# Cross attention's last statistics and projections, and integer attention's third output buffer

## The chip, the cores and the metric

The kernel runs on one core of one Trainium2 chip. The metric is device time in microseconds of one launch, the median of several runs. One run is taken with the hardware profiler; the profile and the trace are of that execution. Engines are named as in the profile: PE is TensorE (PEld its weight loads), DVE is VectorE, ACT is ScalarE, POOL is GpSimd, SP issues the DMAs.

## The reference

A decoder of two levels on x of shape (8, 512, 256), all in float32. Each step adds to x what a block computes of the layer-normalised x:

```python
x = x + L0_attn(layernorm(x))          # self attention, softmax over the queries
x = x + L0_xattn(layernorm(x), ctx)    # 16 heads, scores + adj, integer mask
x = x + L0_ffn(layernorm(x))           # two layers of local attention and gated ffn
x = x + L1_attn(layernorm(x))          # integer attention, values rounded to 8 bits
x = x + L1_xattn(layernorm(x), ctx)    # media attention, 8 heads, masked keys
x = x + L1_ffn(layernorm(x))           # mixture of 8 experts, one per row
```

The change lies in the second and the fourth step. The second, for each batch:

```python
scores  = Q K^T / sqrt(16) + adj
scores  = where(mask == 0, -inf, scores)
out     = softmax(scores) V            # 16 heads of 16
x       = x + out Wo^T + bo
```

The fourth quantises inputs, scores, probabilities and outputs to integers with global scales. Its last product is `attn_int @ wo_int.T + bias_int`, multiplied by a scale for each output column, and added to x.

## The kernel before

x stays in SBUF as 32 tiles of 128 rows by 256, four to a batch. The program is written by hand as stages; a scheduler orders each engine's queue at compile time, by the order in the program, its own model of durations, the tiles' buffers and the dependences. `tc.issue_after(ins)` makes what is written inside it stand behind `ins` on its engine; `high_priority` brings it forward. At run time each engine goes through its queue in order.

**Self attention** (`stage_self_attention`) goes over 8 batches: scores, exponentials, then `weigh`, which for each of four row tiles takes a reciprocal (L1412), a scale (L1413) and a product (L1415) on VectorE and adds the tile to x on GpSimd (L1417). `means(b)` (L1419) computes mean and inverse deviation of the batch's new x for cross attention: for each of four tiles `bn_stats` and `bn_aggr` (L143, L144), then a chain of small instructions on 128x4 elements (L148, L149, L1477 to L1481, L1424), copied into `self.x_ln`. It runs a batch late; the last batch's stands behind the loop (L1445). The bounds check `sa_ok` (L1447 to L1451) ends the stage.

**Cross attention** (`stage_cross_attention`) prepares batch 0 during self attention; its main loop then has 128 steps and two more, 16 steps to a batch. Step i issues, for four heads and one tile of 128 keys: `scores(i)` (four matmuls in two PSUM tiles, L1724), `soften(i)` (two exponentials on ScalarE, L1735, and two multiplications by the mask's share on VectorE, L1736), and `weigh(i - 2)` (four matmuls, L1752). Between them comes side work: the next batch's `prepare` (keys, values, queries, normalised rows: one group a step), and `later`, a list of jobs with due steps: reciprocals of the softmax sums, which go through DRAM (`inverted`, L3330), the multiplication on GpSimd (L1769), the output projection `project_out` (L1785 and L1790) and the statistics of its result. `paced` puts a job behind the VectorE instruction `marks[-2]`, that is, behind the multiplications of the step before. PSUM has six banks for scores, one for `po`, and one, `pj`, that all side work shares. `project_out` multiplies into `pj` and VectorE adds the bank to x:

```python
x = self.x[:, b * NST + i, :]
nc.vector.tensor_tensor(x, x, ps[:, :C], ALU.add)
```

`padded(j, pool)` allocates and clears one of two value buffers, padded to 32 columns a head (GpSimd memset, L1558); odd batches use the second. Toward the end (from step n - 13) the first local attention's preparation (`turn`, `project`, `rotate`, L1881 to L1953) runs between the steps.

**Integer attention** (`stage_quantized_attention`) ends with pool `qa5`: eight activations (L2744) round the attention output, transposes follow (L2748), and after the second of four pairs `bias_parts` splits the bias into three bfloat16 rows on VectorE (L2415 to L2424) and `orow`, the column scales, is written. `bias_parts` allocates its two working rows in a pool of its own. Then for each of 8 batches: 12 matmuls into one of two PSUM tiles (L2764, L2767), `project`, which does a piece of the media attention's keys and values (L2799, stored by a DMA from `kv_o`), a product by `orow` on VectorE into `qa_o` (L2772) and the addition to x (L2773), on GpSimd for batches 2, 4, 6 and on VectorE for the rest. `qa_o` has two buffers of the pool. Batch 0's statistics for the next stage come in between (`twice_normal`), and the others' products stand behind them. The media attention (L2933, L2943, L2963) is the next stage. Its weights are loaded by `load_media_attention` long before.

Of the kernel before, what the change touches and what calls it, by code (L numbers as in the profile page):

```python
# [27 lines left out]
F32 = mybir.dt.float32  # L28
# [1249 lines left out]
class FastDecoder(Decoder):  # L1278
# [31 lines left out]
    def stage_self_attention(self, w, ahead):  # L1310
# [7 lines left out]
        with self.tc.tile_pool(reuse_waits="tile", name="sa", bufs=2) as pool, self.tc.tile_pool(  # L1318
# [97 lines left out]
                    x = self.x[:, at, :]  # L1416
                    nc.gpsimd.tensor_tensor(x, x, o, ALU.add)  # L1417

            def means(b):  # L1419

                x = self.x[:, b * NST : (b + 1) * NST, :]
                at = slice(b * NST, (b + 1) * NST)
                for kept, new in zip(self.x_ln, self.ln_stats(pool, lambda i: [x[:, i, :]], NST, "x_ln")):
                    nc.vector.tensor_copy(kept[:, at], new)  # L1424
# [8 lines left out]
            for b in range(B):  # L1433
# [8 lines left out]
                if b > 0:  # L1442
                    means(b - 1)
                    ahead.step(3)
            means(B - 1)  # L1445
            ok = self.alloc(pool, [P, NT], F32, "sa_ok", bufs=1)
            nc.vector.tensor_scalar(ok, inv, 1.0 / self.SHIFTED_MAX, 1.0 / self.SHIFTED_MIN, ALU.max, ALU.min)  # L1447
            nc.vector.tensor_tensor(ok, ok, inv, ALU.is_equal)  # L1448
# [79 lines left out]
    def stage_cross_attention(self, ahead):  # L1528
# [27 lines left out]
        def padded(j, pool):  # L1556
            v = self.alloc(pool, [P, NST, 16, 32], F32, f"x_v{j}", bufs=1)
            nc.gpsimd.memset(v, 0.0)  # L1558
            nc.gpsimd.memset(v[:, :, :, 0:1], 1.0)
            return v  # L1560
# [30 lines left out]

        def prepare(b):

            d = held[b] = {"v": v_pad[b % 2]}
            own = (first, second)[b % 2]

            def load():
                d["ctxT"] = self.alloc(first, [P, 2, S], F32, "x_ctxT")
                nc.sync.dma_start(
                    d["ctxT"], t["ctxT"].rearrange("(k p) n -> p k n", p=P)[:, :, b * S : (b + 1) * S]  # L1600
                )
                d["mask"] = self.alloc(first, [P, NST, S], I32, "x_mask", bufs=1)
                nc.sync.dma_start(d["mask"], t["x_maskT"][b].rearrange("(k p) q -> p k q", p=P))
                nc.sync.dma_start(
                    self.slots[b * CAP : (b + 1) * CAP, :].rearrange("(p r) c -> p r c", p=P),
                    empty.unsqueeze(1).broadcast_to([P, CAP // P, self.WIDE]),
                )

            def share(k):
                if k == 0:  # L1610
                    d["share"] = self.alloc(own, [P, NST, S], F32, f"x_share{b % 2}", bufs=1)
                nc.vector.scalar_tensor_tensor(
                    d["share"][:, k, :], d["mask"][:, k, :], 0.0, adj[:, k, :], ALU.not_equal, ALU.mult
                )

            x = self.x[:, b * NST : (b + 1) * NST, :]
            normals = [
                lambda i=i: self.normalize(d["xn"][:, i, :], x[:, i, :], self.x_ln, b * NST + i)
                for i in range(NST)
            ]  # L1620

            def behind():
                nc.gpsimd.tensor_tensor(x, x, bias.unsqueeze(1).broadcast_to([P, NST, C]), ALU.add)

            def rows():
                d["xn"] = self.alloc(first, [P, NST, C], F32, "x_xn", bufs=1)
                d["xnT"] = self.alloc(first, [P, 2, S], F32, "x_xnT", bufs=1)
                d["q"] = self.alloc(own, [P, 2, 2, S], F32, f"x_q{b % 2}", bufs=1)
                d["k"] = self.alloc(own, [P, 2, S], F32, f"x_k{b % 2}", bufs=1)

            def turn(c):
                ps = self.pj()
                for i in range(NST):
                    nc.tensor.transpose(
                        ps[:, i * P : (i + 1) * P], d["xn"][:, i, c * P : (c + 1) * P], self.ident
                    )
                nc.scalar.copy(d["xnT"][:, c, :], ps)

            def project(wt, src, g):
                ps = self.pj()  # L1640
                for k in range(2):
                    nc.tensor.matmul(
                        ps, wt[:, k, g * P : (g + 1) * P], src[:, k, :], start=(k == 0), stop=(k == 1)
                    )
                return ps

            def queries(g):
                ps = project(wq, d["xnT"], g)
                for e in range(2):
                    nc.scalar.activation(  # L1650
                        d["q"][:, e, g, :], ps, AF.Identity,
                        bias=qb[:, 2 * e + g : 2 * e + g + 1], scale=qsc[:, e : e + 1],
                    )

            def keys(g):
                ps = project(wk, d["ctxT"], g)
                nc.scalar.activation(d["k"][:, g, :], ps, AF.Identity, bias=bk[:, g : g + 1])

            def values(i):
                ps = self.pj()  # L1660
                for k in range(2):
                    nc.tensor.matmul(
                        ps[:, :C], d["ctxT"][:, k, i * P : (i + 1) * P], wv[:, k, :],
                        start=(k == 0), stop=(k == 1),
                    )
                nc.scalar.copy(
                    d["v"][:, i, :, 1:17], ps[:, :C].rearrange("p (h d) -> p h d", d=16)
                )

            K = [lambda g=g: keys(g) for g in range(2)]  # L1670
            V = [lambda i=i: values(i) for i in range(NST)]
            M = [lambda i=i: share(i) for i in range(NST)]
            T = [lambda c=c: turn(c) for c in range(2)]
            Q = [lambda g=g: queries(g) for g in range(2)]
            yield [load, rows]
            yield []
            yield [K[0]]
            yield []
            yield [K[1]]
            yield [normals[0], normals[1], V[0]]  # L1680
            yield [normals[2], normals[3], V[1]]
            yield [behind, T[0], M[0]]
            yield [T[1], V[2]]
            yield [Q[0], M[1]]
            yield [Q[1]]
            yield [V[3], M[2]]
            yield []
            yield [M[3]]
# [8 lines left out]
        with self.tc.tile_pool(reuse_waits="tile", name="xa", bufs=2) as pool, self.tc.tile_pool(  # L1697
# [2 lines left out]
            second = pool  # L1700
            self.pj = lambda: self.alloc(psum, [P, 512], F32, "pj")
            self.reserve(psum, ("pj", [P, 512], 1), ("po", [P, 512], 1), ("sc", [P, 2, 512], 3))
            v_pad.append(padded(1, pool))

            marks = []

            def paced(thunk):
# [74 lines left out]
            def project_out(b, i):  # L1782
                ps = self.pj()
                for g in range(2):
                    nc.tensor.matmul(  # L1785
                        ps[:, :C], held[b]["oT", g][:, i * P : (i + 1) * P], wo[:, g, :],
                        start=(g == 0), stop=(g == 1),
                    )
                x = self.x[:, b * NST + i, :]
                nc.vector.tensor_tensor(x, x, ps[:, :C], ALU.add)  # L1790
                if i == 0:
                    rows = self.x[:, b * NST : (b + 1) * NST, :]
                    held[b]["norm"] = self.ln_pieces(pool, rows, lambda i: rows[:, i, :], "lt_ln")
                means, roots, normals = held[b]["norm"]
                means[i]()
                if i == NST - 1:
                    nc.sync.dma_start(self.away[b], self.x[:, b * NST : (b + 1) * NST, :])
                    for k, root in enumerate(roots):
                        later.add(1 + k, lambda root=root: paced(root))
                    for k, normal in enumerate(normals):  # L1800
                        later.add(5 + k // 2, lambda normal=normal: paced(normal))
# [11 lines left out]
            for i in range(n + 2):  # L1813
# [13 lines left out]
                later.tick(2)  # L1827
                if i == 1:
                    ahead.step()
                if i == n - 14:  # L1830
                    early.close()
                if i >= n - 13:
# [571 lines left out]
        nc.vector.tensor_tensor(hi, hi, lo, ALU.max)  # L2404
        nc.vector.tensor_tensor(q["xtop"][:, b * NST : (b + 1) * NST], hi, rstd, ALU.mult)

    def bias_parts(self, out, rb, inv, tag):

        nc, part = self.nc, self.ident[:, :3]
        n = rb.shape[1]  # L2410
        with self.tc.tile_pool(reuse_waits="tile", name=tag, bufs=1) as tmp:
            v = self.alloc(tmp, [P, n], F32, tag + "_v")
            acc = self.alloc(tmp, [P, n], F32, tag + "_a")
            piece = self.alloc(tmp, [P, n], BF16, tag + "_p")
            nc.vector.tensor_scalar(v, rb, inv, MAGIC, ALU.mult, ALU.add)  # L2415
            nc.vector.tensor_scalar(v, v, -MAGIC, None, ALU.add)
# [11 lines left out]
    def stage_quantized_attention(self, w):  # L2428
# [3 lines left out]
        with tc.tile_pool(reuse_waits="tile", name="qa", bufs=1) as pool:  # L2432
# [302 lines left out]
            with tc.tile_pool(reuse_waits="tile", name="qa5", bufs=2) as tmp, tc.tile_pool(  # L2735
                reuse_waits="tile", name="qp5", bufs=1, space=PSUM
            ) as psum:
                orow = self.alloc(tmp, [P, C], F32, "qa_orow_s", bufs=1)
                for n in range(0, 8, 2):
                    ps = [self.alloc(psum, [P, 8, P], BF16, "tr", bufs=4) for c in range(2)]  # L2740
                    for h in range(2):
# [13 lines left out]
                                ps[c][:, :, 32 * st : 32 * st + 32].rearrange("p m (k t) -> p t m k", t=B),  # L2755
                            )
                    if n == 2:
                        self.bias_parts(brow, q["rb"][:, 3 * C :], osc_inv, "qa_b")
                        nc.vector.tensor_scalar(orow, q["wsc"][:, C:], osc, None, ALU.mult)
                for b in range(B):  # L2760
                    ps = self.alloc(psum, [P, NST, C], F32, "pj", bufs=2)
# [4 lines left out]
                            )  # L2766
                        nc.tensor.matmul(ps[:, st], ones[:, :P], brow, start=False, stop=True)  # L2767
                    project(tmp, psum, "tr")
                    o = self.alloc(tmp, [P, NST, C], F32, "qa_o")
                    x = self.x[:, b * NST : (b + 1) * NST, :]  # L2770
                    with self.tc.issue_after(ahead) if b else nullcontext():
                        nc.vector.tensor_tensor(o, ps, orow.unsqueeze(1).broadcast_to([P, NST, C]), ALU.mult)  # L2772
# [6 lines left out]
        self.integers.close()  # L2779

    def load_media_attention(self):
        self.w_media = super().load_media_attention()
        return self.w_media

    def context(self, out, b):
# [815 lines left out]
```

## Time and profile before

| what | value |
|---|---|
| time, median of 3 runs | 3000.25 us |
| lowest, highest | 2999.61, 3006.4 us |
| the profiled execution's own time | 2998.56 us |
| its span in the profile | 2996.8 us |
| its mean granted TensorE clock | 0.976 |
| TensorE busy | 2811.1 us (94%) |
| VectorE busy | 2030.6 us (68%) |
| ScalarE busy | 1207.0 us (40%) |
| GpSimd busy | 377.2 us (13%) |

The span runs from the first to the last instruction of the program that was profiled; the own time of the execution is 1.76 us longer. A row of a timeline gives the start (us from the span's start), the length, the engine, the source line, the operation, what it writes and reads, and in brackets the engine's idle time before it and what ended that. Lengths of rows that are merged (x2, x6) hold all of them; on VectorE a row's length reaches a little into the next one, so that costs in a queue are taken from start to start. In stretches: self attention to 205 us, cross attention to about 690, the local transformer's two layers to 2012, integer attention to 2308, media attention to 2760, the experts to the end.

### The profile page before, as it was taken

How to read it: one execution, taken by the hardware profiler on the slowest of the kernel's cores; microseconds unless marked ns; L12 is line 12 of the kernel's file. 1: busy time of each engine (PE TensorE's matmuls, PEld its weight loads, DVE VectorE, ACT ScalarE, POOL GpSimd, SP SyncE). 2: the span in 40 equal slices, each digit the busy share in tenths (PEclk: the TensorE clock that was granted, in tenths of full speed). 3: DMA queues.
4: the chain of work that ended last, by engine and by line, in shares of the span. 5: the costliest groups of instructions: out<-in, count | busy, mean ns of one | idle time of the engine just before them, and what ended most of it. 6: DMA issues, size and time to landing. Idle time of an engine off the chain costs nothing. (4 is left out here: it accounts for less than half of the span.)

```text
span 2996.8 us, 39867 instructions
## 1 busy us (share of the span) xinstructions
PE 2811.1 (94%) x14929; PEld 1509.5 (50%) x14944; DVE 2030.6 (68%) x4514; ACT 1207.0 (40%) x1719; POOL 377.2 (13%) x357
## 2 busy tenths in 40 slices
PE   8999999988999999999999999999796999997998
PEld 5653333324555565655555565555343344444665
DVE  7458999996777883356777888549787766664110
ACT  2227777754545521135445521115263444441111
POOL 1111111100011110000011111112111012121111
PEclk9999999999999999999999999999898999998999
DMA  8011211101000010001000021010332132313331
GB/s 250 1 36 43 78 50 50 58 24 52 16 23 23 23 53 9 1 1 44 16 23 23 23 60 50 15 43 29 121 124 89 48 102 86 107 58 98 112 134 61
DMA packets 130695, 168.74 MB, mean 56 GB/s; under 512 B 51760, under 2 KB 79665, under 8 KB 128442
## 3 DMA queue, kind: packets, MB, share of 16 engines
q1 hardware_dynamic: 126394, 154.48, 16.5%
q0 software_dynamic: 4096, 11.59, 1.0%
q8 instruction: 120, 1.97, 0.3%
q14 instruction: 85, 0.70, 0.1%
HBM read 113.12 MB, written 47.50 MB: 54 GB/s over the span
## 5 line engine op out<-in xcount | busy, mean ns | idle before, releaser
L1897 PE MATMUL pj<-w,la_hT 128*128 128x512 f32 x712 | 333.1, 605 | 8.2 <-DVE x L1790 7.9
L1736 DVE TENSOR_TENSOR x_e<-x_e,x_share 128x1024 f32<-128x1024 f32 x256 | 316.8, 1280 | 14.8 <-ACT x_e L1735 14.7
L1735 ACT ACTIVATE x_e<-sc 128x1024 f32<-128x1024 f32 x256 | 249.2, 1023 | 79.1 <-PE sc L1724 79.1
L2036 DVE TENSOR_TENSOR la_e<-la_e,la_mask 128x1024 f32<-128x1024 f32 (+1 forms) x128 | 137.0, 1084 | 102.9 <-ACT la_e L2035 102.9
L1897 PEld LDWEIGHTS pj<-w,la_hT 128*128 128x128 f32 x712 | 130.3, 191 | 141.1 <-issue 117.1
L2969 ACT ACTIVATE ma_e<-sc,ma_bias 128x1024 f32<-128x1024 f32 x128 | 135.7, 1111 | 143.5 <-PE sc L2963 138.3
L2257 ACT ACTIVATE lf_gate<-pj,lf_b 128x512 f32<-128x512 f32 (+1 forms) x82 | 56.3, 687 | 320.5 <-PE pj L2236 320.5
L3344 POOL TENSOR_TENSOR la_oT<-la_o,x_wide 128x512 f32<-128x512 f32 x64 | 90.4, 1425 | 730.3 <-DMA x_wide<-invs 655.4
L2236 PE MATMUL pj<-lf_hnT,w 128*128 128x512 f32 (+1 forms) x368 | 171.9, 594 | 2.3 <-ACT lf_gate L2257 1.1
L1752 PE MATMUL po<-x_e,x_v 128*32 128x512 f32 x1024 | 138.7, 614 | 22.0 <-DVE x_e L1736 18.1
L2236 PE MATMUL sc<-lf_hnT,w 128*128 128x512 f32 x336 | 157.7, 592 | 0.0
L1724 PE MATMUL sc<-x_q,x_k 32*128 32x512 f32 x1024 | 151.8, 642 | 1.7 <-DVE sa_ok L1448 1.4
L2308 PE MATMUL po<-w,lf_hid 128*128 128x256 f32 x640 | 149.0, 379 | 0.0
L2262 DVE SCALAR_TENSOR_TENSOR lf_hid<-sc,lf_b,lf_gate 128x512 f32<-128x512 f32 x70 | 52.4, 748 | 135.9 <-PE sc L2236 134.7
L2035 ACT ACTIVATE la_e<-sc 128x1024 f32<-128x1024 f32 (+1 forms) x128 | 112.1, 918 | 45.2 <-PE sc L2027 45.2
L2027 PE MATMUL sc<-la_qkT 64*128 64x256 f32 (+1 forms) x1024 | 128.2, 378 | 0.5
L2308 PEld LDWEIGHTS po<-w,lf_hid 128*128 128x128 f32 x640 | 117.8, 190 | 21.2 <-issue 7.4
L2046 PE MATMUL po<-la_e,la_v 128*64 128x256 f32 (+1 forms) x1024 | 121.3, 363 | 7.4 <-ACT la_o L2063 6.5
L2963 PE MATMUL sc<-ma_qT,ma_kT 64*128 64x512 f32 x512 | 127.3, 615 | 0.4 <-ACT ma_e L2969 0.4
L1904 ACT ACTIVATE la_sq<-pj 128x512 f32<-128x512 f32 x120 | 71.8, 598 | 131.2 <-PE pj L1897 129.9
L2986 PE MATMUL po<-ma_e,ma_v 128*64 128x512 f32 x512 | 124.0, 605 | 0.0
L1913 DVE TENSOR_REDUCE la_ss<-la_sq 128x16 f32<-128x1024 f32 x64 | 77.6, 1213 | 66.2 <-ACT la_sq L1904 66.2
(512 smaller groups left out, 5222.7 us busy)
## 6 DMA issues: line engine op xcount, KB each, us to landing
x_wide<-invs SPq DMA_DIRECT2D x184, 128.0 KB
w<-in_f_w_dram SPq DMA_DIRECT2D x16, 1024.0 KB
kv<-kv_o SPq DMA_DIRECT2D x56, 256.0 KB
slots<-x_empty SPq DMA_DIRECT2D x8, 1028.0 KB
x_mask<-in_x_maskT_dram SPq DMA_DIRECT2D x8, 1024.0 KB
ma_kT<-kv SPq DMA_DIRECT2D x8, 1024.0 KB
ma_v<-kv SPq DMA_DIRECT2D x8, 1024.0 KB
ex_rows<-slots SPq DMA_DIRECT2D x7, 1028.0 KB
```

The lines of the kernel that those rows point to most:

```text
L1724: nc.tensor.matmul(pair[r // 2][:, r % 2, :], d["k"][rows, g, kt * P : (kt + 1) * P], d["q"][rows, e, g, :], start=True, stop=True,)
L1735: nc.scalar.activation(ex, d["e"][rest][p], AF.Exp)
L1736: nc.vector.tensor_tensor(ex, ex, d["share"][:, kt, :].unsqueeze(1).broadcast_to([P, 2, 512]), ALU.mult)
L1752: nc.tensor.matmul(d["po"][32 * r : 32 * r + 32, :], d["v"][:, kt, 8 * g + 2 * r + e, :], ex[r // 2][:, r % 2, :], start=(kt == 0), stop=( ...
L1897: nc.tensor.matmul(ps, d["hT"][:, k, i * P : (i + 1) * P], wqkv[:, k, j * S : (j + 1) * S], start=(k == 0), stop=(k == 1),)
L2027: nc.tensor.matmul(both[half][:, r, jj * 256 : jj * 256 + to - j * P], d["qkT"][rows, 4 + c, j * P : (j + 1) * P], d["qkT"][rows, c, j * P ...
L2036: nc.vector.tensor_tensor(ex[:, :, :n_cols], ex[:, :, :n_cols], mask[:, :n_cols].unsqueeze(1).broadcast_to([P, 2, n_cols]), ALU.mult,)
L2236: nc.tensor.matmul(ps[:m, :], w1[:, k, at : at + m], held[b]["hnT"][:, k, :], start=(k == 0), stop=(k == 1))
L2308: nc.tensor.matmul(ps[:, :C], held[b]["hid"][:, f, i * P : (i + 1) * P], w2[:, f, :], start=(f == 0), stop=False,)
L2963: nc.tensor.matmul(both[m // 2][:, r, :], d["k"][rows, c, kt * P : (kt + 1) * P], d["q"][rows, c, :], start=True, stop=True,)
L2969: nc.scalar.activation(ex, ps, AF.Exp, bias=bias[:, b * NST + kt : b * NST + kt + 1], scale=0.125)
L2986: nc.tensor.matmul(d["po"][64 * r : 64 * r + 64, :], d["v"][:, kt, 128 * c + 64 * r : 128 * c + 64 * r + 64], exs[m // 2][:, r, :], start= ...
```

## The change

Cross attention: the statistics of the last batch leave the end of self attention and are issued in step 2 of cross attention's loop, paced, with their small tiles in cross attention's first pool. The second padded buffer is allocated and cleared in the same step, no longer ahead of the loop. `project_out` copies its bank to SBUF on ScalarE, and VectorE adds the copy to x.

Integer attention: `qa_o` has three buffers. For the room, `orow` and the two working rows of the last `bias_parts` take the place of bias rows in `rb` that are no longer needed. The media attention's weights are loaded with the key and value weights ahead of the query weights.

```diff
-            def means(b):
+            def means(b, pool=pool):
...
-            means(B - 1)
+            self.last_means = lambda pool: means(B - 1, pool)
...
         def prepare(b):
-            d = held[b] = {"v": v_pad[b % 2]}
+            d = held[b] = {}
...
             def values(i):
+                d["v"] = v_pad[b % 2]
...
             self.reserve(psum, ("pj", [P, 512], 1), ("po", [P, 512], 1), ("sc", [P, 2, 512], 3))
-            v_pad.append(padded(1, pool))
...
                 x = self.x[:, b * NST + i, :]
-                nc.vector.tensor_tensor(x, x, ps[:, :C], ALU.add)
+                o = self.alloc(pool, [P, C], F32, "x_out")
+                nc.scalar.copy(o, ps[:, :C])
+                nc.vector.tensor_tensor(x, x, o, ALU.add)
...
                 if i == 1:
                     ahead.step()
+                if i == 2:
+                    v_pad.append(padded(1, pool))
+                    paced(lambda: self.last_means(first))
...
-    def bias_parts(self, out, rb, inv, tag):
+    def bias_parts(self, out, rb, inv, tag, room=None):
...
-            v = self.alloc(tmp, [P, n], F32, tag + "_v")
-            acc = self.alloc(tmp, [P, n], F32, tag + "_a")
+            v = room[0] if room else self.alloc(tmp, [P, n], F32, tag + "_v")
+            acc = room[1] if room else self.alloc(tmp, [P, n], F32, tag + "_a")
...
-                orow = self.alloc(tmp, [P, C], F32, "qa_orow_s", bufs=1)
+                orow = q["rb"][:, :C]
...
-                        self.bias_parts(brow, q["rb"][:, 3 * C :], osc_inv, "qa_b")
+                        self.bias_parts(brow, q["rb"][:, 3 * C :], osc_inv, "qa_b", [q["rb"][:, k * C : (k + 1) * C] for k in (1, 2)])
...
-                    o = self.alloc(tmp, [P, NST, C], F32, "qa_o")
+                    o = self.alloc(tmp, [P, NST, C], F32, "qa_o", bufs=3)
...
     def load_media_attention(self):
-        self.w_media = super().load_media_attention()
+        w, t = self.weights(), self.t
+        wkv = self.load_w(w, 1024, t["e_wkv"])
+        self.w_media = self.load_w(w, 0, t["e_wq"]), wkv, self.load_w(w, 3072, t["e_wout"])
         return self.w_media
```

## The prediction

> **What bounds the kernel now.** I read the page, then TensorE's own waits, the windows with the granted clock, and the timelines around the three places that the diff touches. TensorE is busy 94% of the span, so time is won where it waits, and lost where a wait is added.
>
> The page's first lines, then the longest waits of TensorE on the changed lines (total us, times, longest):
>
> ```profile
> span 2996.8 us, 39867 instructions
> PE 2811.1 (94%) x14929; PEld 1509.5 (50%) x14944; DVE 2030.6 (68%) x4514; ACT 1207.0 (40%) x1719; POOL 377.2 (13%) x357
> ...
> PE po L1752 <- DVE x_e L1736: 18.1, 16, 3.7
> PE pj L1897 <- DVE x L1790: 7.9, 2, 4.0
> PE pj L2764 <- DVE qa_o L2772: 6.2, 3, 2.9
> PE pj L2933 <- DVE ma_xn L157: 5.9, 1, 5.9
> PE pj L1785 <- DVE x L1790: 3.8, 7, 0.7
> ```
>
> All these together are 42 us, 1.4% of the span: the change can move no more than a few tenths of a per cent.
>
> The start of cross attention, timeline of VectorE and TensorE (start, length), then windows (PE, PEld, DVE, ACT, POOL busy, granted clock, DMA):
>
> ```profile
> 207.35 0.43 DVE L143 BATCH_NORM_STATS2 x_ln_bn<-x 128x6 f32<-128x256 f32 x1
> ...
> 211.24 6.89 DVE L1736 TENSOR_TENSOR x_e<-x_e,x_share 128x1024 f32<-128x1024 f32 x6
> 213.74 1.93 PE L1752 MATMUL po<-x_e,x_v 128*32 128x512 f32 x8 [3.69 <-DVE x_e L1736]
> 215.60 3.78 PE L1642 MATMUL pj<-x_ctxT,w 128*128 128x512 f32 x4
> ...
> 216.00:218.00 2.00, 2.00 (x3) 0.78 (x3) 2.00 (x2) 0.00 (x0) 0.00 (x0) 0.50 0.00 0
> ```
>
> The exponentials of step 0 are ready at 206.3, but VectorE is at the last statistics until 211.24; TensorE idles 3.69, and the clock is at 0.50 afterwards: the four key matmuls take 3.78 where the same ones take 1.98 at 223.69.
>
> The end of cross attention and the end of integer attention:
>
> ```profile
> 644.66 0.42 DVE L1790 TENSOR_TENSOR x<-x,pj 128x256 f32<-128x256 f32 x1 [1.40 <-PE pj L1785]
> 661.62 0.42 DVE L1790 TENSOR_TENSOR x<-x,pj 128x256 f32<-128x256 f32 x1 [0.61 <-PE pj L1785]
> 655.90 3.40 PE L1897 MATMUL pj<-w,la_hT 128*128 128x512 f32 x4 [3.92 <-DVE x L1790]
> ...
> 2293.56 2.35 DVE L2772 TENSOR_TENSOR qa_o<-pj,qa_orow_s 128x1024 f32<-128x1024 f32 x2 [2.23 <-POOL x L2773]
> 2299.29 2.35 DVE L2772 TENSOR_TENSOR qa_o<-pj,qa_orow_s 128x1024 f32<-128x1024 f32 x2 [2.24 <-POOL x L2773]
> 2305.00 1.23 DVE L2772 TENSOR_TENSOR qa_o<-pj,qa_orow_s 128x1024 f32<-128x1024 f32 x1 [2.23 <-POOL x L2773]
> 2307.97 2.10 PE L2933 MATMUL pj<-ident,ma_xn 128*128 128x128 f32 x8 [5.93 <-DVE ma_xn L157]
> ```
>
> In the first place TensorE stands behind an addition that is queued in VectorE; in the second VectorE stands three times behind GpSimd's addition, which holds an output buffer, and TensorE gets the next stage only when VectorE is through.
>
> **The change part by part. (a) Last statistics to step 2.** VectorE's last rows need 0.17 + 0.16 + 0.48, spaced to 0.9, behind the last matmul of self attention (196.94 + 7.19 = 204.13): done at 205.1 instead of 206.50, since the waits of 0.84 for GpSimd's rows fall away. ScalarE's exponentials of step 0 stay at 205.32 to 207.26, each later step 1.94. Multiplications, 2.3 a step: step 0 from 206.4 to 208.75, so TensorE weighs at 208.8, not 213.74; steps 1 and 2 to 211.1 and 213.5. Then the moved work: four statistics with their sums at 0.6 (136.43 to 136.99 is one) and a chain of 3.2 less 0.9 for which GpSimd's memset held it up, 4.7 in all, to 218.2. Queued behind it are step 3's multiplications, to 220.5, and behind those TensorE's weighing of step 3: 220.6 against 226.67 before, 6.1 earlier, with some 1.2 of waiting left. The memset now falls among these instructions; I charge its 0.9 again: 5.2, **taken as 5.0**. Ceiling: 3.69 + 1.44 of waiting (that at 206.65) and (3.78 − 1.98) + (1.93 − 1.07) of slow clock, 7.8. Floor: 0, if the statistics go ahead of step 2's multiplications and the wait comes back whole. The later buffer of padded values is first written at step 5; its memset (1.81 + 0.20) is on GpSimd, which has nothing else until 230.96; no DMA is among what is moved.
>
> **(b) Projection through ScalarE.** 32 copies at 0.39 (the row of L1666, same shape from PSUM) are 12.5 on an engine that is busy 347 of the stage's 515: beside other work. VectorE's addition from SBUF stays at 0.34 from start to start, as L1790 at 644.66 (next at 645.00); no gain. What changes is when the single bank comes free. Mid-stage TensorE waits 3.8 in 7 batches; each time it waits again a few us later for multiplications behind a reciprocal that waits for its DMA (316.46, 0.78), an anchor that doesn't move: I take 0. At the end the waits of 3.97 and 3.92 vanish (ScalarE is idle from 632 to 642 and from 652 to 659), but VectorE works without a pause from 615.7 to 672.6 except the two idle times shown, 1.40 + 0.61: only these 2.0 come off. The last batch's chain gets one copy longer: −0.3. The addition now reads two SBUF operands, and those stand behind GpSimd's: the two multiplications at 231.00 took 4.53 where 2.36 is usual, while GpSimd added from 230.96 to 233.31. The PSUM-fed L1790 at 306.47 took 0.39 inside GpSimd's 305.47 to 307.60. 2 of the 32 additions now start inside a GpSimd operation; a mean loss of 1.0 (18 multiplications that do) costs 2, a quarter of it on the path: −0.5. **Sum +1.2**; bounds −4 (eight collisions, half of them hidden) and +4 (half of the 3.8 too).
>
> The Trainium skill, page "SBUF — State Buffer", section "SBUF: two separate sides", has this as a rule: an instruction of VectorE with two SBUF inputs and one of GpSimd that reads SBUF take a shared port pair in turn, each for its whole length. The trace agrees with it (4.53 for two multiplications, 0.39 for the PSUM-fed addition). By it this edit trades a bank for a lock.
>
> **(c) Third output buffer.** The product reads PSUM and one SBUF operand, so it can run beside GpSimd, as L1790 did. With a free buffer the waits 2.23 + 2.24 + 2.23 = 6.7 go. What is late next is VectorE's own addition (two SBUF inputs), which would meet GpSimd's three times, up to 1.1 each (2.35 of GpSimd's work from 2291.32, where VectorE's addition ends, less one product of 1.2): 3.4 at worst. Taken 5.0 of 3.4 to 6.7. TensorE's idle 5.93 ahead of L2933 then shrinks to 2 or 3, and its clock, 0.50 there (L2933 2.10 against 1.09, L2943 9.40 against 7.2), may stay up: 0 to 3.2. I take 1.0, because 2.94 of idle at 2291.9 was enough for 0.50 in 2296 to 2298. **Sum 6.0**; bounds 2.2 and 9.9.
>
> The Trainium skill, "TensorE: Matmul & The Clock Gate", section "What's actually happening", has the clock halve after an idle window of some 3.4 us. By it the shorter gap would keep the clock and (c) would be 8.2. The row of 2.94 us speaks against a firm limit there.
>
> **(d) Bias parts and scale in spent rows; order of three weight loads.** VectorE's wait of 1.94 for a store (2262.27) goes, but ScalarE runs five roundings back to back over it (2259.97 for 5.77) and is waited for next: 0 to 1.9, taken 0.3. The weights are issued at 1832 and used first at 2017: 0; their cover is 180 us.
>
> Sum: 5.0 + 1.2 + 6.0 + 0.3 = 12.5. The profiled execution is 2998.56 (span 2996.8 and 1.76 around it): 2986.1. It lies 1.7 under the median, so the median becomes 3000.25 − 12.5 = 2987.8, say 2988.
>
> **The rivals.** *The third buffer moves the wait.* With two buffers the fourth product took the one that GpSimd held, though the other was free at 2291.3; if buffers are still handed out so, one wait of 2.2 goes and (c) is 2.2: 3000.25 − 8.7 = 2991.5. For it: that row. Against: three buffers leave one unused at the first choice. 0.13.
>
> *The start gives it back.* The chain of 14 dependent statistics at 0.2 go ahead of step 2: (a) is 0, 2992.8. For it: VectorE is in order and busy 2.3 of each 3.2. Against: step 2's exponentials are ready by the time the order allows. 0.13.
>
> *Everything pays.* Clock kept in (a) and (c), half of the mid-stage waits won: 6.1 + 3 + 9 + 1 = 19: 2981. 0.12.
>
> *The lock decides.* Each addition meets a GpSimd operation and VectorE, which is full at the end of every batch, hands the 1.0 on: 32 lost, 11.3 won elsewhere: 3021. It is slower than before from 12 collisions on and by over 0.3% from 21. For it: the additions follow GpSimd's multiplication of the same batch. Against: 2 overlaps now. 0.06; that the change has no effect at all through some new order of the instructions, 0.06.
>
> **How the numbers follow.** 0.3%, 9.0 us, is about what a measurement of this kernel can tell from no change. Forecast 0.50, of which 0.42 is over 9.0. Faster: 0.42 + 0.04 + 0.03 + 0.12 = 0.61. Same: 0.08 + 0.09 + 0.10 + 0.05 = 0.32. Slower: 0.06 + 0.01 = 0.07. All bounds at their best give 23.6 (2977), all at their worst −1.8 (3002); leaving out a tenth on each side, 2979 to 2999.
>
> **What would show it.** Right: the first L1752 near 209 with clock 1.00 behind it and x_ln rows among x_e rows; no L1897 wait for L1790, VectorE without idle around 644 and 661; L2772 without a GpSimd wait and L2933 5 us closer to the stage's first product. Wrong: L1790 rows of over 1 us (lock), L2772 still waiting for POOL, or x_e waits at steps 2 to 5 over 3 us.

## The result, and the profile after

The changed kernel takes 2986.47 us (median of 4 runs, 2983.93 to 2989.44); the kernel before, on the same chip, 3001.11 us (2999.61 to 3006.4). The ratio is 0.9952, with a 95% interval of 0.994 to 0.9964: 14.6 us or 0.48% faster by the medians. The forecast was 2988, 12.5 us faster. The profiled execution took 2987.97 (span 2986.1), 10.6 less than that of before (2998.56), and 1.9 more than the 2986.1 that the sum gave for it. The medians differ by 4 us more than the two profiles; why single profiles differ so much turned out to be half of the lesson.

The page's first lines, then TensorE's waits on the changed lines (total us, times, longest). Lines below the edits have moved: L1790 is now ScalarE's copy and L1791 VectorE's addition, L1897 is L1901, L2772/L2773 are L2776/L2777, L2933 is L2939.

```profile
span 2986.1 us, 39956 instructions
PE 2814.6 (94%) x14929; PEld 1510.0 (51%) x14944; DVE 2027.5 (68%) x4514; ACT 1218.2 (41%) x1751; POOL 374.8 (13%) x357
...
PE po L1751 <- DVE x_e L1735: 17.9, 13, 2.6
PE sc L1784 <- POOL x_oT L1768: 6.7, 1, 6.7
PE pj L2939 <- DVE ma_xn L157: 5.7, 1, 5.7
PE pj L2768 <- DVE qa_o L2776: 4.4, 4, 2.1
```

The two waits of the la matmuls for the projection's addition (7.9) are gone from the list, and so is the projection's own wait for it (3.8). The longest wait for x_e is 2.6 instead of 3.7, but all of them together are as long as before (17.9 and 18.1): mid-stage, waits for the addition have in large part turned into waits for x_e. The wait at integer attention's end was expected to shrink to 2 or 3; it is 5.7.

The start of cross attention, timeline of the changed kernel (VectorE, TensorE), then windows (PE, PEld, DVE, ACT, POOL busy, granted clock, DMA share, GB/s):

```profile
206.28 4.63 DVE L1735 TENSOR_TENSOR x_e<-x_e,x_share 128x1024 f32<-128x1024 f32 x4 [0.50 <-ACT x_e L1734]
210.83 0.74 DVE L143 BATCH_NORM_STATS2 x_ln_bn<-x 128x6 f32<-128x256 f32 x2
...
208.55 1.75 PE L1723 MATMUL sc<-x_q,x_k 32*128 32x512 f32 x4 [0.21 <-ACT x_e L1734]
210.23 1.94 PE L1751 MATMUL po<-x_e,x_v 128*32 128x512 f32 x8
212.09 3.78 PE L1642 MATMUL pj<-x_ctxT,w 128*128 128x512 f32 x4
```

```profile
206.00:208.00 2.00, 1.93 (x10) 0.60 (x8) 1.72 (x2) 1.69 (x3) 1.72 (x2) 1.00 0.00 0
...
210.00:212.00 2.00, 2.00 (x10) 0.20 (x8) 2.00 (x7) 1.66 (x2) 0.00 (x0) 0.50 0.00 0
```

Step 0's multiplications now start at 206.28, the statistics come behind those of step 1, and the first weighing starts at 210.23 instead of 213.74. There is no wait of over 0.21 in front of it any more. And yet the clock is at 0.50, and the four key matmuls take 3.78, exactly as before.

The end of cross attention (VectorE's additions, TensorE, then the DMA queue of SP behind the last reciprocal):

```profile
638.40 0.42 DVE L1791 TENSOR_TENSOR x<-x,x_out 128x256 f32<-128x256 f32 x1
649.18 0.42 DVE L1791 TENSOR_TENSOR x<-x,x_out 128x256 f32<-128x256 f32 x1
...
642.79 1.98 PE L1901 MATMUL pj<-w,la_hT 128*128 128x512 f32 x4
650.79 1.06 PE L1751 MATMUL po<-x_e,x_v 128*32 128x512 f32 x8 [2.60 <-DVE x_e L1735]
...
664.53 0.33 SPq L3337 DMA_DIRECT2D invs<-x_inv  x1
667.65 0.32 SPq L1775 DMA_DIRECT2D x_wide<-invs  x1
```

No la matmul waits for an addition, and VectorE doesn't stand idle in front of one. The last two lines are the round trip of the last reciprocal through memory (invs is written, then read back): 3.12 from issue to issue. In the kernel before, the same two stand closer:

```profile
672.69 0.33 SPq L3331 DMA_DIRECT2D invs<-x_inv  x1
674.10 1.71 SPq L1776 DMA_DIRECT2D x_wide<-invs  x4
```

That is 1.41. What stands in between shows in the DMA view of the changed kernel for 663 to 668; the same view of before (671.5 to 675.5) has no second line:

```profile
q1 hardware_dynamic: 144, 0.01, 2.0%
q8 instruction: 1, 0.02, 1.8%
```

One 16 KB packet of instructions is in the record from 665.18 on for 1.43 us, to 666.61. Of the 144 packets that write the reciprocals, 135 are there by 665.6; the other nine come between 666.58 and 666.71, at the end of the instruction packet. In the kernel before, all 144 lie within 0.21 us.

The end of integer attention:

```profile
2282.82 1.23 DVE L2776 TENSOR_TENSOR qa_o<-pj,qw_rb 128x1024 f32<-128x1024 f32 x1 [1.11 <-POOL x L2777]
2287.42 1.22 DVE L2776 TENSOR_TENSOR qa_o<-pj,qw_rb 128x1024 f32<-128x1024 f32 x1 [1.11 <-POOL x L2777]
2290.94 2.12 DVE L2777 TENSOR_TENSOR x<-x,qa_o 128x1024 f32<-128x1024 f32 x1
...
2293.55 2.10 PE L2939 MATMUL pj<-ident,ma_xn 128*128 128x128 f32 x8 [5.71 <-DVE ma_xn L157]
```

Three waits of 2.23 for GpSimd have become two of 1.11; the last addition takes 2.12 instead of 1.22, because it starts inside GpSimd's (2288.72 to 2291.98). From the first product to L2939 it is 25.88 us, where before it was 29.36: 3.5 won.

### The profile page after: what moved, and what is told of

Same layout as the page of the kernel before. It is cut to its first block, busy times and chain, and to the rows that moved or that the text cites. A ratio compares the mean times of both kernels' runs of the same rounds, so it can differ in the third digit from the quotient of the medians.

```text
span 2986.1 us, 39956 instructions
## 1 busy us (share of the span) xinstructions
PE 2814.6 (94%) x14929; PEld 1510.0 (51%) x14944; DVE 2027.5 (68%) x4514; ACT 1218.2 (41%) x1751; POOL 374.8 (13%) x357
## 5 line engine op out<-in xcount | busy, mean ns | idle before, releaser
L1901 PE MATMUL pj<-w,la_hT 128*128 128x512 f32 x712 | 332.0, 603 | 0.3 <-ACT la_hT L1889 0.3
L1735 DVE TENSOR_TENSOR x_e<-x_e,x_share 128x1024 f32<-128x1024 f32 x256 | 313.0, 1265 | 18.2 <-ACT x_e L1734 18.1
L1901 PEld LDWEIGHTS pj<-w,la_hT 128*128 128x128 f32 x712 | 130.4, 191 | 134.0 <-issue 118.9
L1751 PE MATMUL po<-x_e,x_v 128*32 128x512 f32 x1024 | 140.5, 621 | 22.8 <-DVE x_e L1735 17.9
```

The costliest lines, as they stand in the source:

```text
L1735: nc.vector.tensor_tensor(ex, ex, d["share"][:, kt, :].unsqueeze(1).broadcast_to([P, 2, 512]), ALU.mult)
L1751: nc.tensor.matmul(d["po"][32 * r : 32 * r + 32, :], d["v"][:, kt, 8 * g + 2 * r + e, :], ex[r // 2][:, r % 2, :], start=(kt == 0), stop=( ...
L1901: nc.tensor.matmul(ps, d["hT"][:, k, i * P : (i + 1) * P], wqkv[:, k, j * S : (j + 1) * S], start=(k == 0), stop=(k == 1),)
```

## Experiments

**Each part alone.** Three kernels, each the one before with one part of the change. (c) has its spent rows for the bias parts with it, and not the order of the weight loads.

```diff
 e1_stats    last_means and the second padded buffer at step 2 only
 e2_copy     o = alloc(pool, [P, C], F32, "x_out"); scalar.copy(o, ps); vector add from o, only
 e3_third    qa_o with bufs=3, bias parts and scale in q["rb"], only
```

Expected of e1_stats: 

> Part (a) alone: the last statistics and the memset of the padded values at step 2, all else as before. As forecast: 5.0 us faster than before (0 to 7.8). As read from the two traces by now: the first weighing matmul comes 3.5 us earlier than before (210.2 instead of 213.7), and nothing more is won, because TensorE's clock falls to 0.50 here as well, without a long wait, while it is half used: 3.5 us faster, with a spread of some 3 us by how the clock falls. Rival, the start gives it back: the x_e waits of the next steps grow and under 1 us is left.

Expected of e2_copy: 

> Part (b) alone: the projections go through a copy of ScalarE, all else as before. As forecast: 1.2 us faster (4 slower to 4 faster), the waits of TensorE for the projection's addition gone, the mid-stage waits won and given back. As read from the two traces: VectorE's last reciprocal of the stage comes 3 to 4.6 us earlier, some of which the DMA round trip behind it may keep (3.1 instead of 1.4 us in the changed kernel): 2 to 4.5 us faster. Rival, the lock: additions of over 1 us, and slower than before.

Expected of e3_third: 

> Part (c) with the room that it needs, (d): three output buffers, the bias parts and the scale in spent rows; the order of three weight loads as before. As forecast: 6.3 us faster (2.2 to 11.8). As read from the two traces: 3.6 us between the first product and the last addition and 1.0 at the bias parts, 4.5 us in all; two waits of 1.1 for GpSimd stay, the clock is 0.50 at the next stage's first matmuls as before. Rival, the third buffer moves the wait: one wait of 2.2 goes, 2.2 us in all.

Measured against before on one chip (median 3000.87): e1_stats 0.998 (0.9971 to 0.9989), e2_copy 0.9993 (0.9983 to 1.0002), e3_third 0.998 (0.9971 to 0.9989). In us, ratio times 3001: 6.0 (3.3 to 8.7), 2.1 (−0.6 to 5.1), 6.0 (3.3 to 8.7). Together 14.1, and the whole change is 14.4 by its ratio: within these wide intervals the parts add up, and nothing speaks for a gain that needs two of them. Of e2_copy alone no gain is shown, as its interval holds 0. The forecast had 5.0, 1.2 and 6.3.

The trace of e1_stats shows the start without the fall of the clock (timeline, then a window):

```profile
209.81 1.07 PE L1751 MATMUL po<-x_e,x_v 128*32 128x512 f32 x8
210.81 1.98 PE L1642 MATMUL pj<-x_ctxT,w 128*128 128x512 f32 x4
```

```profile
210.00:212.00 2.00, 2.00 (x11) 0.68 (x4) 2.00 (x5) 1.87 (x2) 0.00 (x0) 1.00 0.00 0
```

The same instructions, the same idle times ahead of them (0.21), the clock at 1.00 and L1642 at 1.98. So my theory of 3.5 us for this part, taken from the changed kernel's trace, was too small for this run: by the 400th weighing matmul, counted from the last matmul of self attention, e1_stats was 7.1 us ahead of before, the changed kernel 3.0.

**The memset.** The statistics moved, the memset of the second padded buffer left ahead of the stage.

```diff
-            means(B - 1)
+            self.last_means = lambda pool: means(B - 1, pool)
 ...
+                if i == 2:
+                    paced(lambda: self.last_means(first))
```

> Only the last statistics moved to step 2; the memset of the later padded values stays ahead of the stage, all else as before. As forecast the memset costs 0.9 when it falls among the statistics: the first weighing matmul comes at about 209.8 as in part (a) alone or up to 0.9 later, when VectorE waits for the memset again. If the memset takes no part: the same places as in part (a) alone, 209.8, 213.8, 216.1, 220.1 for the first four weighings, as long as the clock stays at 1.00.

There is one run, and only its trace is read here. The weighings start at 209.77, 213.75, 216.02 and 220.00; in e1_stats at 209.81, 213.79, 216.07 and 220.05. The memset takes no part: in both it runs on GpSimd from 205.9 on, before the first statistic. The forecast's charge of 0.9 was for nothing.

**Two batches instead of eight.** In the kernel with buffers of their own (below), only the last two batches' projections go through ScalarE.

```diff
-                o = self.alloc(pool, [P, C], F32, "x_out")
-                nc.scalar.copy(o, ps[:, :C])
-                nc.vector.tensor_tensor(x, x, o, ALU.add)
+                if b >= B - 2:
+                    (as above)
+                else:
+                    nc.vector.tensor_tensor(x, x, ps[:, :C], ALU.add)
```

> The kernel with buffers of their own, in which only the last two batches' projections go through ScalarE, and the first six batches' additions read PSUM as before. As forecast, the mid-stage is worth 0: the same time within 1.5 us. The three or four additions of 1.16 us or more are gone, the mid-stage waits of TensorE for the addition (3.8) are back and the later waits for multiplications shorter by as much. Rival, the mid-stage pays: 2 to 4 us slower. Rival, the lock costs: 1 to 3 us faster. The round trip behind the last reciprocal, 2.6 to 3.1 us in all kernels with the copy where it is 1.4 in all without it, may be short again: 1.5 us.

2978.26 us against 2978.28 of the kernel with all eight batches on the same chip (5 runs each): the same time, as forecast. But the edit does two things, and the traces don't say that the mid-stage is worth 0. The first is the mid-stage. I take the stretch from the 41st weighing matmul to the fourth-last reciprocal of the stage, in which these copies lie, and compare profiles with the same time at clock 0.50 inside it:

| time at clock 0.50 | with copies | without copies in this stretch |
|---|---|---|
| none | 377.7 (e6_own) | 379.3 (e8_end), 381.8, 382.3 |
| 3.4 us | 379.2, 379.4, 380.1 | 380.8 |
| 6.8 us | 379.3 | 382.6, 382.6, 382.7 |
| 13.7 us | 381.3, 381.9 | (none) |

The entries are the length of the stretch in us. Wherever both kinds stand in a row, the profiles with copies are shorter, e6_own by 1.6 than e8_end, all seven by 1.9 on average than the other seven, though they have more time at 0.50. Profiles with the same code in this stretch scatter by up to 3, so the size is uncertain. TensorE's waits in this stretch tell why: those for the addition (4.1 to 4.5) vanish with the copies, those for x_e grow on the whole, and all together are 16.5 to 19.4 instead of 19.8 to 22.4. The second thing is the round trip below, which wins 1.5 in e8_end. A loss of 1.6 and a gain of 1.5 fit an equal time.

The additions that read two SBUF operands do wait for GpSimd. Durations of the additions (least, median, most, in ns), before and changed:

```profile
L1790 DVE TENSOR_TENSOR x<-x,pj x29: 378/412/422, 303.4 to 680.9; 128x256 f32<-128x256 f32 x29
```

```profile
L1791 DVE TENSOR_TENSOR x<-x,x_out x32: 392/417/1496, 301.1 to 676.8; 128x256 f32<-128x256 f32 x32
```

Read from PSUM, no addition took over 0.43 us, also where it started inside a GpSimd operation. Read from SBUF, three of the changed kernel's 32 took 1.16, 1.50 and 1.17, and each had started inside one; in e8_end, which reads PSUM in those batches, none did. The Trainium skill's rule of the shared port pair ("SBUF — State Buffer", section "SBUF: two separate sides") holds here too, for instructions of VectorE with two SBUF inputs. The three lose 2.6 us in all; what of that reaches the end of the stage isn't measured by itself.

The round trip of the last reciprocal is short again in e8_end:

```profile
659.54 0.33 SPq L3340 DMA_DIRECT2D invs<-x_inv  x1
660.95 1.25 SPq L1775 DMA_DIRECT2D x_wide<-invs  x3
```

It is 1.41. In the fourteen profiles (before, after and the twelve runs), the seven with 32 copies have a 16 KB instruction packet beside this transfer and round trips of 2.4 to 3.1; in each of them the transfer's last nine packets come at the end of the instruction packet. The seven others have none there and 1.41. ScalarE is the engine whose number of instructions differs between e8_end and the kernel with all copies, so it is most likely ScalarE's code that is loaded; the record doesn't say whose it is. From the fourth-last reciprocal of the stage to the next stage's first scores it is 66.8 to 67.2 us without the copies (five profiles), 64.7 to 65.4 with 32 (six, and 64.1 in e7_warm, which has further matmuls there), 63.4 and 64.4 with those of the last two batches only. So some 2 us are won there in the traces, and e8_end wins a further 1.5.

**Whose buffer.** In the changed kernel a product waits for GpSimd although, of three buffers, one is free. GpSimd gets two buffers of its own and VectorE one.

```diff
-                    o = self.alloc(tmp, [P, NST, C], F32, "qa_o", bufs=3)
+                    o = self.alloc(tmp, [P, NST, C], F32, "qa_o%d" % (b if b in (2, 4) else 2 if b == 6 else 1), bufs=1)
```

Run twice, the second time beside the changed kernel:

> The changed kernel, in which GpSimd's products have two buffers of their own and VectorE's one, instead of three that all share: as many buffers, the same order of instructions. Theory: the two waits of 1.1 stay in the changed kernel because a product takes the buffer that was given back last, GpSimd's, though another is free. Then they vanish here, and the next stage begins 2.2 us closer to the first product; some 17 us faster than before instead of 14.6. Rival: the product waits for GpSimd for another reason (the shared port, or x): the two waits stay, and the time is the changed kernel's.

> GpSimd's products in buffers of their own, once more: if the two waits of 1.1 are worth what the trace shows, 2 to 3 us faster than the changed kernel on the same chip.

> The changed kernel once more, beside the next three on one chip: 14 us faster than before; two waits of 1.1 of the products for GpSimd. A second profile of it: the moved grid of the clock's steps gives other stretches of 0.50 than the first (208.9 to 215.8, 2683.6 to 2687.0), the rest of the chain of work is the same.

First chip: 0.9941 (0.9929 to 0.9953) against before, 17.7 us. Second chip: 2978.28 us (2976.31 to 2980.69), the changed kernel 2981.38 (2979.87 to 2983.97), before 2997.53; ratios to before 0.9934 (0.992 to 0.9948) and 0.9946 (0.9932 to 0.996). 3.1 us by the medians, with ranges that just overlap. The second profile of the changed kernel has a span of 2977.9, 8.2 under its first: in it the clock doesn't fall at the start, and the kernel before, measured beside it, is 3.6 faster too by the medians (2997.53 and 3001.11). The trace of e6_own's products is plainer than the times (VectorE):

```profile
2280.83 2.35 DVE L2776 TENSOR_TENSOR qa_o<-pj,qw_rb 128x1024 f32<-128x1024 f32 x2
2283.10 1.22 DVE L2777 TENSOR_TENSOR x<-x,qa_o 128x1024 f32<-128x1024 f32 x1
2284.42 1.23 DVE L2776 TENSOR_TENSOR qa_o<-pj,qw_rb 128x1024 f32<-128x1024 f32 x1
2285.68 1.93 DVE L2777 TENSOR_TENSOR x<-x,qa_o 128x1024 f32<-128x1024 f32 x1
```

No product waits for GpSimd, in either run. From the first product to the end of the last addition: 28.9 us before, 25.4 changed (both profiles of it), 23.2 with buffers of their own (both). The cause is shown: as many buffers, the same order of instructions, only the assignment differs. That the buffer given back last is handed out first is what fits the waits of all kernels here, with two and with three buffers; the traces don't name the buffers.

**The room alone.** Bias parts and scale in spent rows, two output buffers.

> Only the bias parts and the scale moved into spent rows; two output buffers, all else as before. As forecast: 0.3 us (0 to 1.9) from the rounding scale's reciprocal to the first product; as read from the changed kernel's trace: 1.0. The three waits of 2.2 for GpSimd stay. One look at the trace is enough, the time itself is within its scatter.

There is one run, and only its trace is read. From the reciprocal of the scale to the first product it is 21.4 us, before 21.8, changed 20.7 and 20.8 (e3_third 21.1). So the room alone brings 0.4, near the forecast's 0.3. The 1.0 that I had read from the changed kernel's trace isn't all due to the room: where the rest comes from, no run tells. The four profiles without the room have 21.8 to 22.0 here, those with room and three buffers 19.6 to 21.1, so the difference of 0.6 to 0.7 between this run and the changed kernel is within the scatter. The waits stay as they were:

```profile
2299.40 2.35 DVE L2772 TENSOR_TENSOR qa_o<-pj,qw_rb 128x1024 f32<-128x1024 f32 x2 [2.23 <-POOL x L2773]
```

**Is the clock a matter of how busy TensorE is?** Matmuls whose results nobody reads fill long waits, in the kernel with buffers of their own.

```diff
 e7_warm   project_out, last batch, last row:
+                    for k in range(20):
+                        nc.tensor.matmul(ps[:, :C], held[b]["oT", 0][:, :P], wo[:, 0, :], start=True, stop=True)
           after the last product:
+                        for k in range(32):
+                            nc.tensor.matmul(busy[:, :C], mT[:, 0, 0, 0], wT[:, 0, 3 * C :], start=True, stop=True)
 e9_warm2  instead, after the last product only (late is the buffer of batch 6's product, the last but one):
+                        for k in range(14):
+                            nc.tensor.matmul(busy[:, :C], self.ident, late[:, k % NST, :], start=True, stop=True)
 e10_both  e9_warm2's edit in e8_end
```

> The kernel with buffers of their own, and matmuls whose results nobody reads in two of TensorE's long waits: 20 of 128x256 f32 ahead of the last batch's projections (a wait of 7.6), 32 of 128x256 bf16 behind the last product of integer attention (a wait of 4.5). Theory: the clock is set in steps of 3.41 us, and falls after a step in which TensorE was busy for less than about half; the waits themselves stay, but the clock stays at 1.00 behind them: L2939's eight matmuls take 1.1 instead of 2.1 and the sixteen behind them 7.2 instead of 9.0, 3 us there and 2 us behind the projections: 3 to 5 us faster than the kernel with buffers of their own. Rival: the clock falls for another reason, or the extra matmuls stand in the way: no gain, or a loss of up to 2 us.

> The kernel with buffers of their own, with 14 matmuls of 128x256 f32 whose result nobody reads, behind the last product of integer attention. Unlike the 32 before, which landed between the products, they read the sixth product, so that they can't start before it is there. Theory (steps of 3.41 us, clock falls after a step in which TensorE was busy for less than half): the wait of 4.5 ahead of media attention shrinks to under 1.5 and the clock stays at 1.00 there: the eight L2939-like matmuls take 1.1 instead of 2.1, the sixteen behind them 7.2 instead of 9.0, media attention's first scores come some 2.8 us earlier after the first normalised rows, and the time is 2 to 3 us below the kernel with buffers of their own. Rival: the clock goes by something else than how long TensorE was busy, and falls as before: no gain.

> The same 14 matmuls in the kernel whose first six batches add from PSUM and only the last two go through ScalarE. If the two edits are independent: the same time as with the 14 matmuls alone, within 1.5 us, some 22 us faster than before.

e7_warm: 2978.14 us beside 2978.28, no gain. Its first filling worked: the wait of 7.6 ahead of the last projections was filled, no stretch of 0.50 begins there (in e6_own one does, at 663, two steps long), and the next stage starts 1.0 earlier, of which the round trip (2.4 instead of 2.9) has half. The second was issued between the products instead of behind them, a wait of 3.1 remained and the clock fell. e9_warm2 put that right, by data that come late. Its timeline, TensorE:

```profile
2289.86 6.21 PE L2787 MATMUL tr<-qa_o,ident 128*128 128x256 f32 x28
2296.13 1.09 PE L2945 MATMUL pj<-ident,ma_xn 128*128 128x128 f32 x8
```

and windows:

```profile
2294.00:2296.00 2.00, 2.00 (x10) 1.49 (x8) 2.00 (x9) 0.00 (x0) 0.22 (x1) 1.00 0.19 78
2298.00:2300.00 2.00, 1.98 (x5) 0.99 (x6) 2.00 (x10) 0.00 (x0) 0.00 (x0) 1.00 0.00 0
```

The eight matmuls take 1.09 where they take 2.10 in the changed kernel, and the clock stays at 1.00 through 2300: it goes by how busy TensorE is. But each of the 14 became two instructions of 0.22, 6.2 us in all, so the stage started 1.6 us late (25.2 from the first product to the first matmul of media attention, 23.6 without the filling). Of the 2 to 3 us expected, about 1 is left in the trace at media attention's first scores (34.2 from the first product, 35.2 without the filling), and none in the time: 0.9939 (0.9927 to 0.9952) against before, 18 us. e10_both has 0.9939 (0.9926 to 0.9952): the same as e9_warm2, as expected, but 18 us and not the 22 that were expected. Fewer of them would be the next try; that wasn't run.

No version beats the one with buffers of their own by more than the scatter: e6_own, e7_warm and e8_end lie within 0.14 us of each other on one chip, 19 us under before.

## Why the prediction was right, and where it was not

**(a) Last statistics, 5.0 of 0 to 7.8: right in size, wrong on the clock.** The walk held. Weighing of step 3 was put at 220.6; e1_stats has 220.05. The first was put at 208.8 and came at 209.8, since TensorE was still at step 2's scores until then. "With clock 1.00 behind it" is the step that failed: ten profiles have this part, and in five the clock stays up (7.1 to 8.1 us ahead of before by the 400th weighing matmul, about the ceiling of 7.8), in one it falls for one step (6.4), in four for two (3.0 to 4.2, the changed kernel's first profile among them). The mean of the ten is 5.7, and the time of the part alone 6.0. The rival that the start gives it back is out. The memset's 0.9 was the other wrong step, and too small to matter.

**(b) Projections through ScalarE, +1.2 of −4 to +4: 2.1 (−0.6 to 5.1) by the time, with wrong terms.** Mid-stage was taken as 0, because each wait for the addition was to come back as a wait for multiplications. That step failed: only part of it comes back, and the traces with copies are some 2 us shorter there; e8_end's equal time hid it, since its shorter round trip wins 1.5. At the end, 2.0 was taken for VectorE's two idle times: measured 3.2 from the fourth-last to the last reciprocal (56.8 to 53.6). The term was mis-sized because the idle that a late projection causes isn't 2.0 but 3.1: in the profile of before one multiplication (639.85, 2.22 long) happened to meet GpSimd and covered 1.0 of it, and in e12_room, where none does, VectorE stands idle 3.1. The copy in the last batch's chain was taken at 0.3 and cost nothing that shows (5.0 from the start of GpSimd's last multiplication to the next stage's scores, before and changed); what cost was the instruction packet at the round trip, 1.0 to 1.7, which no part of the sum had foreseen. At the stage's end the two errors nearly cancel: about 2 is left. The lock, 2 of 32 in the forecast, was 3 of 32 (2 to 4 in the seven profiles with copies).

**(c) Third buffer, 6.0 of 2.2 to 9.9: too high, 3.5 in the trace.** The step that failed is that with a third buffer all of the 6.7 goes. Two waits of 1.1 stay, and the last addition loses 0.9 to the port (1.1 was named as the most for one): 6.7 − 2.2 − 0.9 = 3.6. The rival that the wait moves had the mechanism but not the price: it had two waits of 2.2 left, and there are two of 1.1. And the idle ahead of L2939 didn't shrink to 2 or 3, since TensorE's own last products come earlier by 3.3 of the 3.5; so the clock was 0.50 there as before, and the 1.0 taken for it was 0. e9_warm2 shows that a clock of 1.00 was to be had, and that filling the wait gives the gain away again.

**(d) Bias parts, 0.3 of 0 to 1.9: 0.4 for the room alone.** The weight order at 0 wasn't tried by itself.

**The sum.** 5.0 + 1.2 + 6.0 + 0.3 = 12.5 was forecast; the parts measured by themselves give 6.0 + 2.1 + 6.0 = 14.1, where the last 6.0 holds (c) and (d) and is 4.2 in its trace. The two profiles alone would have given 10.7: before's profile is one of two in fourteen in which the clock doesn't fall behind media attention's wait for ma_oT (3.77, clock 1.00 at 2696; in the changed kernel the wait is 3.87 and the clock falls at 2683.6), and the changed one loses 2.9 in that stage, which the change doesn't touch; in integer attention's middle, just as untouched, it wins 2.3 (the twelve runs: −0.1 to 3.6). Scatter of this kind, some 3 us in a profile, is half of the change's largest parts and more than its smaller ones. That the sum came so near is in part luck: by the traces (c) was 2.5 too high, and (b)'s mid-stage some 2 too low.

## What to carry to other kernels

More buffers help only if the slow reader's buffer isn't the next to be handed out: look for who released the wait that is left, and give each reader's engine its own. A copy that frees a PSUM bank early paid at the end of the stage here, and by the traces mid-stage too, although the wait came back in part a few us later, for another reason. Two kernels with equal times need not be equal in each stage: a gain and a loss of 1.5 us each can hide in them, so compare stage by stage. When single waits of 2 to 4 us are at stake, read several profiles: whether a wait also costs clock is decided by where it falls on a grid that the kernel doesn't control.

## What the runs showed of the hardware

In the fourteen traces every stretch at clock 0.50 (but the last, cut off by the end) lasts a multiple of 3.413 us, and all stretches of one run begin on one grid of 3.413 us, whose place differs from run to run. The fine windows of the changed kernel show a fall that follows no long wait (PE busy, clock, DMA share, GB/s):

```profile
208.00:208.50 0.50, 0.34 (x2) 1.00 0.00 0
208.50:209.00 0.50, 0.45 (x2) 0.93 0.00 0
209.00:209.50 0.50, 0.50 (x4) 0.50 0.00 0
...
215.50:216.00 0.50, 0.50 (x5) 0.74 0.00 0
```

It falls at 208.93 and rises at 215.76, two steps later. I laid each trace's grid over TensorE's matmul records and took, for every step between 10 and 2960 us that ran at full clock, the share of it in which at least one matmul was under way. Of 203 steps with a share under 0.42, 200 were followed by 0.50; of 150 between 0.42 and 0.58, 55; of 11188 above, 16. Of those 16, five are the step ahead of this fall, with a share of 0.92, but with score matmuls of 32 of the array's 128 rows that run two at a time, where at 203.90 four run side by side: counted by rows, the step is used to 0.55. That rows count isn't shown, though: before and e2_copy have a step of 0.51 and 0.53 by rows at the same place (0.66 and 0.69 by time), and no fall behind it. The other eleven lie at 2703 to 2725, ahead of media attention's routing, with shares of 0.69 to 0.84; why the clock falls there stays open. So in all but these 16 what goes ahead of a fall is a step of the grid in which TensorE is at work for less than about half of the time. A wait of 2.94 can lower the clock, since it lies in one step (share 0.17); one of 3.77 need not, since it is spread over two (0.42 and 0.47). The Trainium skill ("TensorE: Matmul & The Clock Gate", section "What's actually happening") has the window of 3413 ns and that it runs freely; the traces agree. That it takes a whole idle window, as I used that section, they don't.

The second thing was the instruction packet: in seven profiles nine of the 144 packets of an 8 KB write come only when a 16 KB packet of instructions (0.96 to 1.43 us) ends, and the round trip is 1.0 to 1.7 us longer. So code that an engine loads can stand in the way of data. The packet's place moved when ScalarE had 24 copies fewer.
